# Sums of x2 with the rows of a1 and a3 for the last four token tiles: made in the second FFN group, one per item, in place of four at a time in the third

## The chip, the cores and the metric

The kernel runs on one core of one Trainium2 chip. The metric is the device time of one execution in microseconds (us). Its engines work side by side, each through its own queue in order: PE (TensorE, matrix products; PEld is its loading of weights), DVE (VectorE), ACT (ScalarE), POOL (GpSimd) and SP, which here starts nearly all DMAs.

## The reference, cut to what matters

The input is x of shape 2 x 1024 x 1024, that is 2048 tokens of width 1024. Two blocks follow each other; the first (gate, up, top-k, down) ends in x1 below, and only the second is touched.

```python
x1 = layernorm(x + attn_block(x, w_gate, w_up, w_down))
def qlora(x, wq, A, B):               # rank 2
    return x @ tile(wq, (1, 4)).T + (x @ A.T @ B.T) * 0.5
gate = silu(qlora(x1, w1q, a1, b1)); up = qlora(x1, w3q, a3, b3)
out  = layernorm(x1 + qlora(gate * up, w2q, a2, b2))
```

The rank-2 term of gate and up needs x1 @ a1.T and x1 @ a3.T: for each token four sums of 1024 products, one for each row of a1 and a3. These "sums", 0.5 times the product included, are what the change moves, for the tokens of the last four tiles. The width-1024 input is also folded four times to width 256, since wq is tiled four times.

## The kernel before, in words

**Tiles and groups.** The 2048 tokens are 16 tiles (0 to 15) of 128 tokens, in four groups of four (0 to 3). x1, called x2 in the code, is kept in DRAM as x_d[t]. The FFN runs group by group (`ffn(g)`, L854 on; group 1 is the second FFN group, group 2 the third). The inner width 2752 is cut into eight blocks b of 344. In the second half of the kernel the trace has for each group an f1 stage (32 items, one for each block and tile) and an f2 stage (the second product and layernorm, four items).

**One f1 item** (`f1_mm`, L958 on) is: PE makes 14 matmuls (L981 to L984) into one of three pairs of PSUM banks; ACT makes the silu of the gate half (L987); DVE multiplies it with the up half (L988), which frees the PSUM pair, and multiplies the product with two rows of a2 into a buffer pa (L990); ACT sums both halves of pa (L992, with its short reads of the accumulator); from block 2 on POOL adds the product to hf (L994).

**Preparing a tile for the next group** (`f1_tile`, L915 on) comes at the start of the even blocks, a tile each: SP loads x2 (L920); for tiles 12 to 15 alone, four times, DVE multiplies x2 with a row of a1 or a3 into a buffer pr (L925) and ACT sums it into `dall` (L926); POOL folds x2 (L927 to L929); DVE makes small copies of the four sums (L931 to L940). `f1_tile2` later transposes the result on PE (L949, L951). For the other tiles the sums come from the stages before the FFN (`dots_down`, `f1_first`).

**Buffers.** pr and pa share one tag with two buffers (`tag="pr", bufs=2`), given out in the order of the source. x2a has two buffers, gt three, PSUM pairs three.

**Order of the work.** `item` (L150 on) keeps a short line of pending items, so that the code of an item's matmuls follows four steps behind the step that calls it in the f1 stage. A planner of the framework (`schedule_with_timeline_sim=True`) then places the instructions on the queues from a timeline of its own, with the order of the source as preference. What an engine finds in its queue is then run strictly in that order.

Of the kernel before, what the change touches and what calls it, by code (L numbers as in the profile page):

```python
# [7 lines left out]
F = mybir.dt.float32  # L8
# [5 lines left out]
ALU = mybir.AluOpType  # L14
AF = mybir.ActivationFunctionType
# [3 lines left out]
P = 128  # L19
H = 1024  # L20
# [12 lines left out]
GT = 4  # L33
# [32 lines left out]
class Kern:  # L66
# [748 lines left out]
    def dots_down(self):  # L815
# [6 lines left out]
                self.nc.sync.dma_start(ab[i], self.A[("a1", "a3")[i // 2]][i % 2 : i % 2 + 1, :].partition_broadcast(P))  # L822
        yield from self.dots(range(2 * GT), [xt[:, 0:H], xt[:, H : 2 * H]], ab, jk[:, :H])

    def dots(self, tiles, xs, ab, jk):
        def load(t):
            with self.load_behind():
                self.nc.sync.dma_start(xs[t % 2], self.x_d[t])

        load(tiles[0])  # L830
        for t in tiles:
            for i in range(4):
                yield
                if i == 0 and t + 1 in tiles:
                    load(t + 1)
                with self.behind():
                    self.nc.vector.scalar_tensor_tensor(
                        jk, xs[t % 2], 0.5, ab[i], ALU.mult, ALU.mult, accum_out=self.dall[:, t, i : i + 1]
                    )
# [14 lines left out]
    def ffn(self, g):  # L854
        tiles = [t for t in range(g * GT, (g + 1) * GT) if t < self.nt]
        for b in range(NB):
            ws = []
            if tiles[-1] + 1 < self.nt:
                if b % 2 == 0:
                    if b:  # L860
                        self.f1_tile2(tiles[-1] + b // 2)
                    self.f1_tile(tiles[-1] + 1 + b // 2)
            for t in tiles:
                self.item(
                    lambda: self.f1_prep(b, ws),
                    lambda: None,
                    lambda st=self.fst[t], b=b, ws=ws: self.f1_mm(st, b, ws),
                    2, 2,
                )
        if tiles[-1] + 1 < self.nt:  # L870
            self.f1_tile2(tiles[-1] + GT)
        ws = []
        for t in tiles:
            self.item(
                lambda: self.f2_w(ws),
                lambda t=t: self.f2_prep(self.fst[t], t),
                lambda st=self.fst[t], t=t, ws=ws: self.f2_mm(st, t, ws),
                2, 1,
            )
# [35 lines left out]
    def f1_tile(self, t, f=None):  # L915
        nc, fp, sm = self.nc, self.fp, self.sm
        V, G = nc.vector, nc.gpsimd
        st = self.fst[t] = {}
        x2 = fp.tile([P, H], F, tag="x2a", bufs=2, name="x2a")
        nc.sync.dma_start(x2, self.x_d[t])  # L920
        d = self.dall[:, t]
        f = f or fp.tile([P, 2 * P], F, tag="fold", bufs=1, name="fold")
        for i in range(4 if t >= 3 * GT else 0):
            pr = self.fp2.tile([P, H], F, tag="pr", bufs=2, name="pr")
            V.tensor_tensor(pr, x2, self.abc[:, i, :], ALU.mult)  # L925
            nc.scalar.activation(pr, pr, AF.Copy, scale=0.5, accum_out=d[:, i : i + 1])  # L926
        G.tensor_tensor(f, x2[:, 0:256], x2[:, 256:512], ALU.add)  # L927
        G.tensor_tensor(f, f, x2[:, 512:768], ALU.add)
        G.tensor_tensor(f, f, x2[:, 768:1024], ALU.add)  # L929
        dr = sm.tile([P, 4], R, tag="dr", name="dr")  # L930
        V.tensor_copy(dr, d)  # L931
        tl = fp.tile([P, P + 6], F, tag="tl", bufs=1, name="tl")
        G.memset(tl, 0.0)
        d2 = d.rearrange("p (w r) -> p w r", w=2)
        dr2 = dr.bitcast(F).rearrange("p (w r) -> p w r", w=2)
        for w in range(2):
            q = 38 * w
            V.tensor_copy(tl[:, q : q + 2], dr2[:, w])
            V.tensor_copy(tl[:, q + 2 : q + 4], dr2[:, w])
            V.tensor_tensor(tl[:, q + 4 : q + 6], d2[:, w], dr2[:, w], ALU.subtract)  # L940
        st["f"] = f, tl
# [150 lines left out]
```

## Time and profile before

| what | us |
|---|---|
| median of 3 runs (lowest to highest) | 1923.47 (1922.35 to 1924.25) |
| the profiled execution: its own time | 1926.91 |
| the profiled execution: span from the first instruction to the last | 1925.1 |
| f1 stage of group 1, first matmul to last (1589.2 to 1662.7) | 73.5 |
| f1 stage of group 2 (1696.9 to 1775.4) | 78.5 |
| f1 stage of group 3 (1810.6 to 1882.7) | 72.1 |
| L925, the sums on DVE (128 x 1024), 16 of them: lowest / median / highest | 1.209 / 1.219 / 1.953 |
| L926, the sums on ACT, 16 of them: median, and 0.186 for the read of the accumulator | 1.060 |
| L994, POOL's add to hf, 96 of them: lowest / median / highest | 0.904 / 1.612 / 1.913 |

A page of the profile gives busy time by engine, and groups of instructions by source line. A timeline lists single instructions: start, duration, engine, line, operation, tiles, and in brackets how long the engine had been idle and what it waited for. "Waits" add such idle time up by pairs. "Windows" give busy time of each engine in a stretch. Durations of neighbours on one engine can overlap by some hundredths of a us, so the step from start to start is the better measure of what an instruction costs its queue.

### The profile page before, as it was taken

Reading aid. Unit: us, or ns where it says so; the run is one execution under the profiler, and the core shown is the slowest. Engines: PE = TensorE matmul, PEld = TensorE weight load, DVE = VectorE, ACT = ScalarE, POOL = GpSimd, SP = SyncE. Lnnn points to the kernel's source line nnn. Section 1 sums busy time; section 2 is a strip of 40 time slices with the busy share of each in tenths; the row PEclk is TensorE's granted clock in tenths of the full one; section 3 lists DMA queues with packets and bytes.
Section 4 is the critical chain, followed back from the end, with each engine's and each line's share of the span. In section 5 each row is a group of like instructions: output and inputs, shape, how many; then the busy total and the mean of one; then the engine's idle time right before and its main releaser. Section 6 shows DMA issues by size and latency. Waiting matters only on the chain. (4 is left out here: it accounts for less than half of the span.)

```text
span 1925.1 us, 29381 instructions
## 1 busy us (share of the span) xinstructions
PE 1885.3 (98%) x10825; PEld 1754.4 (91%) x10825; DVE 1229.6 (64%) x1831; ACT 904.0 (47%) x1448; POOL 973.0 (51%) x606
## 2 busy tenths in 40 slices
PE   9999999999999999999999999999998999998998
PEld 9999999999999999999888787888787979898896
DVE  4633556767358574691238998688467857779565
ACT  4333477414883258622246533323333746557362
POOL 5655664445445354355565443554565746436062
PEclk9999999999999999999999999999999999999999
DMA  7677687676977868667798756977776878485651
GB/s 266 237 250 260 236 325 261 210 272 253 330 231 241 314 235 303 236 228 256 282 328 285 270 188 227 337 245 261 268 250 244 279 284 321 155 318 177 229 196 66
DMA packets 166205, 488.66 MB, mean 254 GB/s; under 512 B 24772, under 2 KB 45380, under 8 KB 166056
## 3 DMA queue, kind: packets, MB, share of 16 engines
q1 hardware_dynamic: 165848, 486.43, 71.9%
q8 instruction: 85, 1.39, 0.3%
q14 instruction: 64, 0.52, 0.1%
q10 hardware_dynamic: 208, 0.31, 0.0%
HBM read 370.30 MB, written 116.33 MB: 253 GB/s over the span
## 5 line engine op out<-in xcount | busy, mean ns | idle before, releaser
L174 POOL TENSOR_TENSOR wl<-wr,wh 128x1376 fp32r<-128x1376 f32 (+2 forms) x187 | 566.4, 3035 | 466.1 <-ACT wh L173 436.8
L353 PE MATMUL mm<-wh,xh 128*128 128x344 f32 x1928 | 610.4, 322 | 2.8 <-DMA wh<-tw3T1h 2.8
L353 PE MATMUL mm<-wh,xl 128*128 128x344 f32 x1928 | 609.8, 320 | 0.0
L173 ACT CAST wh<-wr 128x1376 fp32r<-128x1376 f32 (+2 forms) x192 | 232.4, 1215 | 340.9 <-PE mm L353 199.6
L353 PEld LDWEIGHTS mm<-wh,xh 128*128 128x128 f32 x1928 | 364.7, 189 | 3.0 <-issue 3.0
L353 PEld LDWEIGHTS mm<-wh,xl 128*128 128x128 f32 x1928 | 364.6, 189 | 0.0
L353 PE MATMUL mm<-wl,xh 128*128 128x344 f32 x1928 | 342.1, 319 | 0.0
L353 PEld LDWEIGHTS mm<-wl,xh 128*128 128x128 f32 x1928 | 310.1, 188 | 0.0
L765 PE MATMUL mm<-wh,mh 128*128 128x512 f32 x680 | 217.8, 400 | 0.1
L765 PE MATMUL mm<-wl,mh 128*128 128x512 f32 x680 | 215.1, 395 | 1.1 <-POOL wl L174 1.1
L765 PE MATMUL mm<-wh,ml 128*128 128x512 f32 x648 | 205.5, 396 | 0.8 <-DVE ml L750 0.8
L460 ACT ACTIVATE jk<-a,cur 128x2752 int8<-128x2752 f32 x66 | 170.8, 2588 | 31.2 <-DVE cur L482 15.8
L994 POOL TENSOR_TENSOR hf<-hf,gt 128x344 f32<-128x344 f32 x96 | 142.2, 1491 | 75.6 <-DVE gt L988 68.7
L725 POOL TENSOR_TENSOR m<-m,ub 128x512 f32<-128x512 f32 (+2 forms) x93 | 111.0, 1194 | 128.0 <-ACT ub L724 65.8
L981 PE MATMUL mm<-wh,fh 128*128 128x344 f32 x512 | 166.2, 325 | 5.8 <-DVE gt L988 5.2
L983 PE MATMUL mm<-wh,fl 128*128 128x344 f32 x512 | 164.0, 320 | 0.0
L982 PE MATMUL mm<-wl,fh 128*128 128x344 f32 x512 | 163.9, 320 | 0.0
L765 PEld LDWEIGHTS mm<-wl,mh 128*128 128x128 f32 x680 | 127.4, 188 | 30.1 <-POOL wl L174 2.2
L768 DVE TENSOR_TENSOR acc<-acc,mm 128x1024 f32<-128x1024 f32 x96 | 116.4, 1214 | 57.9 <-PE mm L765 27.8
L765 PEld LDWEIGHTS mm<-wh,mh 128*128 128x128 f32 x680 | 124.7, 189 | 24.8 <-ACT mh L749 0.5
L765 PEld LDWEIGHTS mm<-wh,ml 128*128 128x128 f32 x648 | 121.2, 189 | 26.9 <-DVE ml L750 1.0
L992 ACT ACTIVATE pa<-pa 128x344 f32<-128x344 f32 x256 | 123.0, 483 | 38.6 <-DVE pa L990 34.0
(191 smaller groups left out, 2742.5 us busy)
## 6 DMA issues: line engine op xcount, KB each, us to landing
wr<-wu SPq DMA_DIRECT2D x64, 688.0 KB
wr<-wg SPq DMA_DIRECT2D x52, 688.0 KB
wr<-wd SPq DMA_DIRECT2D x48, 512.0 KB
s_d<-cc SPq DMA_DIRECT2D x64, 344.0 KB
m_d<-mt SPq DMA_DIRECT2D x64, 344.0 KB
a<-s_d SPq DMA_DIRECT2D x64, 344.0 KB
wl<-wc_w SPq DMA_DIRECT2D x48, 344.0 KB
wh<-wc_w SPq DMA_DIRECT2D x48, 344.0 KB
```

Of the source, the lines that this page charges most:

```text
L173: self.lasta = self.nc.scalar.copy(hi, raw)
L174: (eng or self.nc.gpsimd).tensor_tensor(lo, raw, hi.bitcast(F), ALU.subtract)
L353: self.nc.tensor.matmul(o, l, r, start=start and n < m and n % (2 * KH) == 0, stop=stop and n >= m and (n - m) % KH == KH - 1)
L460: nc.scalar.activation(jk.bitcast(I8), av[j], AF.Sign, bias=t, scale=-1.0, accum_out=s)
L725: nc.gpsimd.tensor_tensor(m[:, :w], m[:, :w], ub[:, :w], ALU.mult)
L765: nc.tensor.matmul(ps[:, h], a, b[:, h * 512 : (h + 1) * 512], start=i == 0, stop=i == len(ops) - 1)
L768: nc.vector.tensor_tensor(out, out, ps.rearrange("p a b -> p (a b)"), ALU.add)
L981: nc.tensor.matmul(o, fh[:, c, :], wh[:, c, :], start=c == 0, stop=False)
L982: nc.tensor.matmul(o, fh[:, c, :], wl[:, c, :], start=False, stop=False)
L983: nc.tensor.matmul(o, fl[:, c, :], wh[:, c, :], start=False, stop=False)
L992: nc.scalar.activation(pa[:, r], pa[:, r], AF.Copy, scale=0.5, accum_out=part[:, r, b : b + 1])
L994: G.tensor_tensor(hf[:, hs], hf[:, hs], gt, ALU.add)
```

## The change

The four sums leave `f1_tile`. A generator `dots3` makes them: for each tile from 12 on it loads x2 into an x2a buffer, and with each call makes one sum, a product on DVE and a sum on ACT as before. It is created at the start of block 0 of group 1, and called once before each item of the odd blocks; four odd blocks with four items each make the 16 sums. `f1_tile` for tiles 12 to 15, in group 2, still loads x2 for the folds.

```diff
+    def dots3(self):
+        for t in range(3 * GT, self.nt):
+            x2 = self.fp.tile([P, H], F, tag="x2a", bufs=2, name="dx")
+            self.nc.sync.dma_start(x2, self.x_d[t])
+            for i in range(4):
+                d, pr = self.dall[:, t, i : i + 1], self.fp2.tile([P, H], F, tag="pr", bufs=2, name="pr")
+                self.nc.vector.tensor_tensor(pr, x2, self.abc[:, i, :], ALU.mult)
+                self.nc.scalar.activation(pr, pr, AF.Copy, scale=0.5, accum_out=d)
+                yield
...
+            if (g, b) == (1, 0):
+                self.dg = self.dots3()
             for t in tiles:
+                if b % 2:
+                    next(self.dg, None)
                 self.item(
...
         f = f or fp.tile([P, 2 * P], F, tag="fold", bufs=1, name="fold")
-        for i in range(4 if t >= 3 * GT else 0):
-            pr = self.fp2.tile([P, H], F, tag="pr", bufs=2, name="pr")
-            V.tensor_tensor(pr, x2, self.abc[:, i, :], ALU.mult)
-            nc.scalar.activation(pr, pr, AF.Copy, scale=0.5, accum_out=d[:, i : i + 1])
```

## The prediction, made before the changed kernel was built

> **What bounds the kernel.** I read the page first, then the windows of the f1 stages of groups 1, 2 and 3, then PE's waits and the timelines of DVE, POOL and ACT in them. The page:
>
> ```profile
> span 1925.1 us, 29381 instructions
> PE 1885.3 (98%) x10825; PEld 1754.4 (91%) x10825; DVE 1229.6 (64%) x1831; ACT 904.0 (47%) x1448; POOL 973.0 (51%) x606
> ```
>
> PE bounds the kernel; only idle time of PE can be won or lost. The three f1 stages, in order (stretch, its length, busy time of PE, PEld, DVE, ACT, POOL, granted clock, DMA share, GB/s):
>
> ```profile
> 1589.20:1662.70 73.50, 73.50 (x473) 73.20 (x472) 53.93 (x104) 47.44 (x157) 47.94 (x43) 1.00 0.77 276
> 1696.90:1775.40 78.50, 74.87 (x473) 73.23 (x472) 72.31 (x110) 59.38 (x180) 43.03 (x37) 1.00 0.73 245
> 1810.60:1882.70 72.10, 72.10 (x459) 71.89 (x458) 47.17 (x76) 45.55 (x155) 37.81 (x26) 1.00 0.65 228
> ```
>
> Groups 1 and 2 make the same matmuls (x473). Group 1 does it in 73.5 us with PE never idle; group 2 takes 78.5, and its DVE is busy for 72.3 of them. In group 2 PE waits (total, times, longest):
>
> ```profile
> PE mm L981 <- DVE gt L988: 3.6, 5, 1.7
> ```
>
> The rest of the 5.0 us is the pipeline running dry and refilling at five stalls. The sums stand right there. DVE at the last of the four bursts:
>
> ```profile
> 1749.56 1.95 DVE L925 TENSOR_TENSOR pr<-x2a,abc 128x1024 f32<-128x1024 f32 x1
> 1751.43 0.50 DVE L988 TENSOR_TENSOR gt<-gt,mm 128x344 f32<-128x344 f32 x1
> 1751.85 3.09 DVE L925 TENSOR_TENSOR pr<-x2a,abc 128x1024 f32<-128x1024 f32 x2
> 1754.86 0.50 DVE L988 TENSOR_TENSOR gt<-gt,mm 128x344 f32<-128x344 f32 x1
> 1755.28 1.21 DVE L925 TENSOR_TENSOR pr<-x2a,abc 128x1024 f32<-128x1024 f32 x1
> 1756.42 1.60 DVE L990 TENSOR_TENSOR pa<-gt,ab 128x688 f32<-128x688 f32 x1
> 1757.94 0.50 DVE L988 TENSOR_TENSOR gt<-gt,mm 128x344 f32<-128x344 f32 x1
> ```
>
> and POOL beside it:
>
> ```profile
> 1752.00 1.85 POOL L994 TENSOR_TENSOR hf<-hf,gt 128x344 f32<-128x344 f32 x1 [1.58 <-DVE gt L988]
> 1755.44 1.85 POOL L994 TENSOR_TENSOR hf<-hf,gt 128x344 f32<-128x344 f32 x1 [1.59 <-DVE gt L988]
> ```
>
> POOL's add takes 0.904 alone but 1.85 here, and L990 1.60 in place of its usual 0.87: one waits while the other runs. With DVE's queue full, each add of POOL costs DVE about 0.75 (1.60 less 0.87). Now DVE and POOL in group 1, undisturbed:
>
> ```profile
> 1643.27 0.51 DVE L988 TENSOR_TENSOR gt<-gt,mm 128x344 f32<-128x344 f32 x1 [0.78 <-ACT gt L987]
> 1643.81 0.87 DVE L990 TENSOR_TENSOR pa<-gt,ab 128x688 f32<-128x688 f32 x1
> 1645.47 0.52 DVE L988 TENSOR_TENSOR gt<-gt,mm 128x344 f32<-128x344 f32 x1 [0.78 <-ACT gt L987]
> ```
>
> ```profile
> 1643.86 1.61 POOL L994 TENSOR_TENSOR hf<-hf,gt 128x344 f32<-128x344 f32 x1 [0.59 <-DVE gt L988]
> ```
>
> An item takes PE 2.20 us (1643.27 to 1645.47). DVE needs 1.42 and idles 0.78, but POOL's add runs in that very gap: it ends at 1645.47.
>
> **What is removed.** Twelve of the 16 sums lie inside group 2's f1 stage, four (1666 to 1671) in the f2 stage of group 1. Without them group 2's f1 stage should run as group 1's does now: 78.5 - 73.5 = **5.0 us won**. The four in f2 hide nothing: PE has no idle time after 1663.8 there, so they give back 0. PE also waits 0.8 for DVE (L1029) as group 2's f2 begins; I count it as 0 and keep 0.8 for the range. ACT's 12 x (1.06 + 0.19) go too; no wait of PE names them.
>
> **What is added.** Sixteen products on DVE and sixteen sums on ACT, all in group 1's f1 stage. With the line of pending items, the sums of block 1's calls stand before items of block 0, and so on: tile 12 in block 0, 13 in block 2, 14 in block 4, 15 in block 6. The order of pr and pa pins them: in group 2 the pa of item 4 (L990) came only after the burst, though its L988 had run.
>
> One product steps DVE's queue by 1.14 (1755.28 to 1756.42): 16 x 1.14 = 18.2. In blocks 2, 4 and 6, 12 products stand beside a POOL add, 12 x 0.75 = 9.0. Together 27.2 against DVE's idle time in that stage, 73.5 - 53.9 = 19.6. So 7.6 are lacking. Some of this is queue: how late may L988 be before PE stops? At 1734.10 PE had waited 1.75, for an L988 that I put 5.05 late (started 1733.55, its item's matmuls done at 1727.9, usual delay 0.6): PE tolerates **3.3**. 7.6 - 3.3 = 4.3.
>
> The same walked item by item: L988, product and L990 with POOL's add take 3.08 (1754.86 to 1757.94), so each item of a called block falls 0.88 behind; the first falls 0.75 + 1.14 - 0.78 = 1.1, as the gap is POOL's. Four: 3.7, which is 0.4 over; in the next block DVE regains 2.20 - 1.33 = 0.87 per item and is level. So 0.4 for each of blocks 4 and 6, 1.4 for block 2 (L988 begins there at 1614.1 after a gap of 1.9 and three more follow closely; the fourth would stand 3 x 3.22 later, 3.22 being L988's step 0.54, L990's 0.79, POOL's 0.75 and the product's 1.14, and end at 1624.3, where PE needs its pair at 1636.1 - 6 x 2.20 = 1622.9, counted back from the steady items), and an estimate of 0.9 for block 0, where DVE is already busy with the last layernorm of group 0 (9.0 of 10 us from 1590). Sum 3.1; folds of POOL that come later, as tiles 9 to 11 now have one x2a buffer in turn with `dots3`, add about 0.8 (one more wait of 0.75). I take **4.2 lost**, near both 4.3 and 3.9; the ends are 0 (all fits the gaps) and 7.6 (no queue to draw on).
>
> ACT: 1.30 an item in steady state, 2.4 with a sum, against 2.20; 0.8 over four items, below DVE's lag. The new loads: four of 0.5 MB. SP's queue now waits at them for a free x2a buffer, with the weights of the next block behind; those have a block of 8.8 us in hand, so 0; without that cover, the price of rival three. Tile 13's load waits for tile 12's products (about 1603) and its first product stands at about 1609; in group 1 an x load issued at 1582.8 let DVE go on at 1588.5, 5.7 later. It just fits.
>
> A rule of the Trainium skill bears on POOL's waits. "SBUF — State Buffer", section "Who interferes with whom", says that a DVE instruction with two SBUF inputs and a GpSimd instruction that reads SBUF exclude each other for the whole instruction, whoever begins first. The rows agree with exclusion (L990 0.87 or 1.60), but by the rule the price would be a whole add, 0.90 for 0.75: 12 x 0.15 = 1.8 more lost, an estimate from that page. "Perfetto Trace Analysis", section "Optimizing Scalar/DVE Operations", says that where DVE causes bubbles though it is not saturated, smaller pieces help; by that the loss would be near 0, but no run here shows it, and group 1's DVE would be close to saturated.
>
> **Sum.** -5.0 + 4.2 = -0.8 on the profiled execution, 1926.91 to 1926.1 (its span and the 1.8 around it). It stands 3.4 above the median of the runs; the same difference on 1923.47 gives **1922.7**.
>
> **Rivals.**
>
> 1. *Fits the gaps, faster.* If products fall where POOL is not waiting, an item takes 1.33 + 1.14 = 2.47 and falls 0.27 behind; four make 1.1, far below 3.3, and PE never stops. For it: DVE has 19.6 idle. Against: POOL's add fills that gap in every steady item. Loss 0 to 1: net -4 to -5, and -5.8 with f2's 0.8. About 1919.0.
>
> 2. *ACT in the wrong order, slower.* If the planner puts the sum of an item (L926) ahead of the silu (L987) of the item whose PSUM pair PE needs, each late product holds the silu: 1.14 + 1.15 (ACT) + 0.46 (L987) + 0.51 (L988) + 0.79 (L990) + 0.75 (POOL) = 4.8 an item. The lag is 2.8, then 2.6 each, 10.6 less 3.3 = 7.3 in each of three blocks and about 4 in block 0: 26 lost, net +21; if half the items stand so, +8. It decides where the product ends after its item's matmuls. For it: the order at 1751.5 is L926 before L987, twice. Against: in steady items ACT idles 0.80 until the matmuls of an item end, so that its silu is ready before a late product is. 1931 to 1944.
>
> 3. *Late load, slower.* Tile 13's or 14's x2 lands after DVE has reached its product; L988 stands behind. 5.7 less the lag PE bears, twice: +5, about 1928.5.
>
> 4. *Nothing moves.* Pinned by the pr order, the sums could run later than meant; the bursts then stay bursts, and the time stays within 1 us of before.
>
> **Chances.** My case 0.42; rival one 0.27; rival two 0.24; rival three 0.05; rival four 0.02. A measurement of this kernel can tell about 0.2%, 3.8 us, from no change. My case and rival four are within it (0.44), rival one faster (0.27), two and three slower (0.29). The range goes from 5.8 won, 1917.7, to 1938, which leaves out the worse half of rival two (0.12) and little below. The likeliest case's own range, from its ends (0 to 7.6 lost), is 1918.5 to 1926.1.
>
> **What would show it.** L925 at 16 places in 1590 to 1660 and none after 1665; group 2's f1 stage at 73.5; DVE in group 1's f1 stage near 72 busy; L990 and L925 there near 1.6 and 1.9 beside L994; PE waiting for L988 in blocks 0, 2, 4 and 6. I am wrong if PE has no idle time in group 1 (rival one), if ACT waits for L925 with a silu behind (two), or if L925 waits for a DMA (three).

## Result, and the profile after

The changed kernel takes 1929.64 us (median of 6 runs, 1924.01 to 1932.12) against 1922.91 for the kernel before (6 runs, 1919.90 to 1924.25). The ratio is 1.0034, with a 95% interval of 1.0019 to 1.0049: the change costs 6.7 us. 1922.7 was predicted, with a gain of 0.8.

The page of the profile after:

```profile
span 1922.2 us, 29388 instructions
PE 1883.6 (98%) x10825; PEld 1754.0 (91%) x10825; DVE 1227.5 (64%) x1831; ACT 903.8 (47%) x1448; POOL 975.6 (51%) x606
```

**A trap comes first.** This profiled execution took 1924.01, which is 2.9 *less* than the profiled execution of before, though the medians say 6.7 more. The part ahead of the FFN differs: the first L994 matmul of group 0 (L984 before) starts at 1462.82, against 1471.57, with the same instructions in the same order on every engine, the semaphore records apart. In the 14 profiled executions of this study that part takes between 1462.8 and 1471.6. So two whole spans can't be compared here, but two FFNs can. From that matmul to the end it is 453.53 before and 459.38 after, 5.85 more, close to the 6.7 of the medians. All stage lengths below run from the first to the last L994 of the stage (f1) and from there to the first one of the next (f2).

| kernel | f1.0 | f2.0 | f1.1 | f2.1 | f1.2 | f2.2 | f1.3 | f2.3 | FFN |
|---|---|---|---|---|---|---|---|---|---|
| before | 79.80 | 38.79 | 72.24 | 35.47 | 77.23 | 36.41 | 70.84 | 42.75 | 453.53 |
| after | 80.02 | 38.45 | 80.78 | 38.60 | 72.28 | 35.50 | 70.84 | 42.91 | 459.38 |
| difference | +0.2 | -0.3 | **+8.5** | **+3.1** | **-4.95** | **-0.9** | 0 | +0.2 | +5.85 |

"f1.1" is the f1 stage of group 1. The gain in group 2 is there, 5.9 with f2; the loss in group 1 is 11.7, where 4.2 was forecast. Here are the windows of the f1 stages of groups 1, 2 and 3, as in the prediction, with group 1's f2 stage as the second line (stretch, length, busy time of PE, PEld, DVE, ACT, POOL, granted clock, DMA share, GB/s):

```profile
1580.30:1662.70 82.40, 76.11 (x474) 73.16 (x473) 78.38 (x125) 61.13 (x183) 45.16 (x42) 1.00 0.80 278
1662.70:1699.70 37.00, 34.32 (x152) 27.60 (x152) 20.03 (x52) 10.45 (x30) 7.44 (x16) 0.95 0.41 145
1699.70:1773.30 73.60, 73.60 (x473) 73.21 (x472) 50.36 (x95) 47.00 (x157) 44.39 (x38) 1.00 0.74 256
1807.50:1879.70 72.20, 72.20 (x460) 71.94 (x459) 47.21 (x76) 45.57 (x155) 37.88 (x26) 1.00 0.66 227
```

Group 2 now runs as group 1 did before (73.6, PE never idle). Group 1 is worse than group 2 ever was: 82.4, with DVE busy for 78.4 of it. PE's waits in that f1 stage:

```profile
PE mm L991 <- DVE gt L998: 4.9, 6, 1.6
PE tp L959 <- POOL fold L939: 1.2, 1, 1.2
```

and in the f2 stage behind it:

```profile
PE mm L765 <- ACT hh L1038: 2.7, 1, 2.7
```

The same wait for hh was 0.76 before. It is the last items of f1, late, that f2 needs. The wait of 1.2 ended by a fold is POOL's lateness in its own right: the last fold of tile 9 began only at 1609.8, among adds, as its x2 had come late (POOL waited 9.0 for it).

Now DVE in block 6 of group 1, where one product goes with each item (start, duration, engine, line, operation):

```profile
1645.86 1.75 DVE L831 TENSOR_TENSOR pr<-dx,abc 128x1024 f32<-128x1024 f32 x1
1647.54 0.50 DVE L998 TENSOR_TENSOR gt<-gt,mm 128x344 f32<-128x344 f32 x1
1648.13 0.99 DVE L1000 TENSOR_TENSOR pa<-gt,ab 128x688 f32<-128x688 f32 x1
1649.04 1.95 DVE L831 TENSOR_TENSOR pr<-dx,abc 128x1024 f32<-128x1024 f32 x1
1650.91 0.50 DVE L998 TENSOR_TENSOR gt<-gt,mm 128x344 f32<-128x344 f32 x1
1651.52 1.63 DVE L1000 TENSOR_TENSOR pa<-gt,ab 128x688 f32<-128x688 f32 x1
1653.08 1.21 DVE L831 TENSOR_TENSOR pr<-dx,abc 128x1024 f32<-128x1024 f32 x1
```

and POOL in the same stretch ("x2" puts two adds together):

```profile
1646.49 3.42 POOL L1004 TENSOR_TENSOR hf<-hf,gt 128x344 f32<-128x344 f32 x2
1651.49 0.93 POOL L1004 TENSOR_TENSOR hf<-hf,gt 128x344 f32<-128x344 f32 x1 [1.58 <-DVE gt L998]
```

No line of DVE has a bracket: it waits for no other engine's result, one instruction follows the other. Yet L831 takes 1.75 and 1.95 in place of 1.21, and L1000 1.63 in place of 0.87. The second of POOL's two adds ends at 1649.91, inside the product that starts at 1649.04 and takes 0.74 too long; the add of 1651.49 runs undisturbed in 0.93, and the L1000 that starts with it, at 1651.52, takes 0.76 too long. The product of 1653.08 meets no add and takes 1.21. From one L998 to the next it is 3.37 and 3.3, where PE's item takes 2.20. ACT beside it:

```profile
1647.65 1.06 ACT L832 ACTIVATE pr<-pr 128x1024 f32<-128x1024 f32 x1 [0.56 <-DVE pr L831]
1648.61 0.19 ACT L832 ACTIVATION_READ_ACCUMULATOR pr<-pr 128x1 f32 x1
1648.70 0.44 ACT L997 ACTIVATE gt<-mm 128x344 f32<-128x344 f32 x1
```

The sum (L832) does stand before a silu (L997), as rival two feared. But that silu ends at 1649.14, and DVE comes to its next L998 only at 1650.91: DVE is later still.

### The profile page after: what moved, and what is told of

Its sections match the earlier page's. It is cut to its first block, busy times and chain, and to the rows that moved or that the text cites. A ratio compares the mean times of both kernels' runs of the same rounds, so it can differ in the third digit from the quotient of the medians.

```text
span 1922.2 us, 29388 instructions
## 1 busy us (share of the span) xinstructions
PE 1883.6 (98%) x10825; PEld 1754.0 (91%) x10825; DVE 1227.5 (64%) x1831; ACT 903.8 (47%) x1448; POOL 975.6 (51%) x606
## 5 line engine op out<-in xcount | busy, mean ns | idle before, releaser
L174 POOL TENSOR_TENSOR wl<-wr,wh 128x1376 fp32r<-128x1376 f32 (+2 forms) x187 | 568.6, 3047 | 471.8 <-ACT wh L173 459.9
L1004 POOL TENSOR_TENSOR hf<-hf,gt 128x344 f32<-128x344 f32 x96 | 141.8, 1487 | 73.5 <-DVE gt L998 71.8
L765 PEld LDWEIGHTS mm<-wh,mh 128*128 128x128 f32 x680 | 124.3, 188 | 24.5 <-ACT mh L749 0.4
```

Source lines behind the costliest of these rows:

```text
L174: (eng or self.nc.gpsimd).tensor_tensor(lo, raw, hi.bitcast(F), ALU.subtract)
L765: nc.tensor.matmul(ps[:, h], a, b[:, h * 512 : (h + 1) * 512], start=i == 0, stop=i == len(ops) - 1)
L1004: G.tensor_tensor(hf[:, hs], hf[:, hs], gt, ALU.add)
```

## Experiments

Theories at the start. **B**: products of DVE and adds of POOL keep each other out, so that the 12 sums beside adds (blocks 2 to 7) each cost about 1 us. **A**: the x2a buffers, now shared with `dots3`, push the folds of tiles 9 to 11 late (they run at 1602 to 1611, 1625 to 1630 and 1642 to 1647), and late folds put POOL, and then DVE, behind. **C**: ACT, as in rival two. Diffs are against the changed kernel, but for the eleventh. Each stage length is from one profiled execution. The changed kernel has two (after and e12): f1.1 differs by 1.1 between them and f2.1 by 0.95, so single differences of about 1 us say nothing. The ratio is to the kernel before, with its 95% interval.

| run | ratio | f2.0 | f1.1 | f2.1 | f1.2 | f2.2 | FFN |
|---|---|---|---|---|---|---|---|
| before | 1 | 38.79 | 72.24 | 35.47 | 77.23 | 36.41 | 453.53 |
| after | 1.0034 [1.0019, 1.0049] | 38.45 | 80.78 | 38.60 | 72.28 | 35.50 | 459.38 |
| e1 no sums | 0.9990 [0.9977, 1.0002] | 39.88 | 74.07 | 35.48 | 72.27 | 35.52 | 451.75 |
| e2 own x2 buffer | 1.0094 [1.0071, 1.0116] | 38.95 | 94.4 | 37.24 | 72.28 | 35.53 | 471.56 |
| e3 one SBUF input | 1.0018 [1.0005, 1.0031] | 38.97 | 76.57 | 39.04 | 72.27 | 35.50 | 456.16 |
| e4 sum on DVE | 1.0022 [1.0012, 1.0032] | 40.89 | 80.50 | 40.13 | 72.29 | 35.47 | 462.12 |
| e5 x2 in the weight ring | 1.0053 [1.0034, 1.0073] | 40.92 | 83.80 | 40.42 | 72.27 | 35.53 | 465.58 |
| e6 no POOL add | 0.9962 [0.9948, 0.9976] | 38.86 | 72.64 | 33.95 | 72.29 | 35.50 | 446.75 |
| e7 bursts of four | 1.0016 [1.0006, 1.0026] | 39.09 | 78.44 | 38.02 | 72.85 | 35.51 | 456.65 |
| e8 sums in f2 | 1.0066 [1.0051, 1.0081] | 39.49 | 82.96 | 40.39 | 72.30 | 35.53 | 465.4 |
| e9 split | 0.9976 [0.9965, 0.9986] | 38.76 | 73.87 | 35.47 | 72.44 | 35.52 | 449.32 |
| e10 split, weight ring | 0.9984 [0.9975, 0.9994] | 39.72 | 75.08 | 35.49 | 72.27 | 35.53 | 450.9 |
| e11 no POOL add, before | 0.9987 [0.9976, 0.9999] | 38.74 | 72.48 | 33.93 | 74.61 | 37.07 | 450.37 |
| e12 after, again | 1.0032 [1.0018, 1.0047] | 38.91 | 81.87 | 37.65 | 72.28 | 35.51 | 459.9 |

### 1. The gain alone: no sums at all

```diff
-                self.dg = self.dots3()
+                self.nc.gpsimd.memset(self.dall[:, 3 * GT :, :], 0.0)
...
-                if b % 2:
-                    next(self.dg, None)
```

> Leaves out the 16 sums of the last four tiles altogether (they are set to 0), in both places. Measures what taking them out of group 2 brings by itself. Both theories: group 2's f1 stage at 72.2 to 72.4 us from the first L994 to the last (77.2 before the change, 72.3 after it) and group 1's at 72.2 as before the change; time 5 to 6 us under the kernel before (ratio 0.997). If the ratio stays at 1.000, the stages of the profile do not add up to the time.

Measured: 0.9990. f1.2 and f2.2 gain just what they gain in the changed kernel (-4.96 and -0.9), and group 1 is near its old time. So nearly all of the loss in group 1 is the sums' own. The whole, -1.8 in the profile, misses the 5 to 6 expected, as f1.0, f2.0 and f1.1 are each 1.1 to 1.8 longer here. In f1.1 it is one stall of 1.58 at 1623.5, where DVE had stood behind POOL's memset of tl. In f2.0 the granted clock is 0.50 for 6.8 us (from 1554.1), where it is so for 3.4 us in the kernel before. In f1.0 PE waits 6.8 in place of 4.4; why, isn't known.

### 2. Theory A: another buffer for the new loads

```diff
-            x2 = self.fp.tile([P, H], F, tag="x2a", bufs=2, name="dx")
+            x2 = self.fp2.tile([P, H], F, tag="x2", bufs=2, name="dx")
```

> The changed kernel with the x2 of the sums loaded into the two buffers of f2's x2, so that the folds keep both x2a buffers. Theory A (the folds of POOL came late through the shared x2a buffers, into the blocks where POOL also adds, and each costs DVE a wait of about 0.75): six to nine folds go back ahead of block 2, group 1's f1 stage falls from 80.8 to 75 to 77 and the time by 4 to 6 us against the changed kernel. Theory B (the products and POOL's adds alone fill DVE): f1 stage still 79 to 81. Theory C (ACT's sums hold the silu): as B.

Measured: 1.0094, worse, and by a new mechanism. The buffer x2 is also that of the f2 stage, here group 0's; the first product runs only at 1607.4, and the pa of the first items stand behind it on DVE, so that PE stood for 13.5 us at one place. This run says nothing on A, as f1.1 is another stage altogether; experiment 5 tries another buffer.

### 3. Theory B: a product with a single SBUF input

DVE halves x2 and sums it in one instruction, without the rows of a1 and a3.

```diff
-                self.nc.vector.tensor_tensor(pr, x2, self.abc[:, i, :], ALU.mult)
+                self.nc.vector.tensor_scalar(pr, x2, 0.5, None, ALU.mult, ALU.add, accum_out=d)
```

> The changed kernel with each product made as x2 times 0.5, an operation with one input from SBUF (the row of a1 or a3 is left out, so the sums are others). Same number of instructions on DVE, ACT, POOL. Theories A and B (DVE and POOL exclude each other when DVE reads two inputs from SBUF): no product is stretched beyond 1.3 us by POOL, the adds of POOL beside them go from 1.85 to about 0.95, group 1's f1 stage falls to 75 to 77. Theory C (ACT) or plain length of DVE's work: 80 to 81 as in the changed kernel.

Measured: f1.1 is 4.2 shorter than after (76.57), f2.1 is 39.04, as late as after; 1.0018. DVE's groups in the f1 stage of group 1 (busy us, mean ns | idle before), in the profile after:

```profile
L1000 DVE TENSOR_TENSOR pa<-gt,ab 128x688 f32<-128x688 f32 x22 | 25.8, 1174 | 0.8
L831 DVE TENSOR_TENSOR pr<-dx,abc 128x1024 f32<-128x1024 f32 x15 | 23.9, 1592 | 0.0
```

The same two groups in this run:

```profile
L1000 DVE TENSOR_TENSOR pa<-gt,ab 128x688 f32<-128x688 f32 x22 | 27.6, 1258 | 0.9 <-ACT pr L832 0.2
L831 DVE TENSOR_SCALAR_CACHE_REDUCE pr<-dx 128x1024 f32<-128x1024 f32 x15 | 18.1, 1207 | 0.0
```

and pa alone in the changed kernel's second profile (experiment 12):

```profile
L1000 DVE TENSOR_TENSOR pa<-gt,ab 128x688 f32<-128x688 f32 x21 | 26.3, 1258 | 0.7
```

From the changed kernel to this one the products lose their stretch altogether (1592 to 1207 ns). So half of B holds: a product with two SBUF inputs waits for POOL, one with a single input doesn't. The multiplication into pa, untouched by the edit, keeps its stretch. Its mean is higher than in the profile after (1258 against 1174), but the unaltered kernel's second profile has 1258 too; that waiting passes from the products on to pa isn't shown. The Trainium skill, "SBUF — State Buffer", section "Who interferes with whom", has this very distinction: a DVE instruction with two SBUF inputs contends with a GpSimd instruction that reads SBUF, one with a single input, outside the two-port modes, doesn't. The means here agree with it (1592 against 1207).

### 4. Theory C: the sum without ACT

```diff
-                self.nc.vector.tensor_tensor(pr, x2, self.abc[:, i, :], ALU.mult)
-                self.nc.scalar.activation(pr, pr, AF.Copy, scale=0.5, accum_out=d)
+                self.nc.vector.scalar_tensor_tensor(pr, x2, 0.5, self.abc[:, i, :], ALU.mult, ALU.mult, accum_out=d)
```

> The changed kernel with each sum made on DVE alone (product and sum in one instruction, about 1.22 plus 0.08 by L837), nothing on ACT. Theory C (ACT's 1.15 per sum holds the silu or the buffers of pr): group 1's f1 stage falls from 80.8 to 76 or less. Theories A and B: 80 to 82, since DVE has 16 times 0.08 more and waits for POOL as before.

Measured: f1.1 80.50 against 80.78, and the whole 1.0022, with an interval that overlaps that of after. ACT without a single sum leaves f1.1 where it was, so C falls, and rival two with it.

### 5. Theory A again: x2 in the ring of weight buffers

```diff
-            x2 = self.fp.tile([P, H], F, tag="x2a", bufs=2, name="dx")
+            x2 = self.wr.get()[:, :H]
```

> The changed kernel with the x2 of the sums loaded into the ring wr, which is idle after group 0, so that the folds keep both x2a buffers and no load of the sums waits for f2. Theory A (folds of POOL that came late cost DVE waits): POOL makes the folds of tiles 9 to 12 ahead of block 3 again, group 1's f1 stage falls from 80.8 to 76 to 78, time 3 to 5 us under the changed kernel. Theory B (products against POOL's adds alone): 79.5 to 81.

Measured: 1.0053; f1.1 is 83.80, longer than after by 3.0, though the folds, which no longer wait for a buffer that `dots3` holds, all lie between 1592.9 and 1614.4. So early folds don't bring the time back. The run doesn't say more than that: the first products now stand beside folds and are stretched as well (1.70 to 1.76 at 1595.1 and 1601.9), and 1.1 of the 3.0 is no more than lies between the changed kernel's two profiles. What settles A is experiment 6.

### 6. Theory B: no adds of POOL in group 1

Items of group 1 leave out POOL's add to hf.

```diff
-        st = self.fst[t] = {}
+        st = self.fst[t] = {"add": t // GT != 1}
...
-        if b >= 2:
+        if b >= 2 and st.get("add", True):
```

> The changed kernel without POOL's add to hf in group 1 (the output of group 1's tokens lacks six of eight blocks). Theory B (each add costs DVE about 0.75 beside a product; 12 of them 9.0): group 1's f1 stage falls from 80.8 to 73 to 75 and the wait at the start of its f2 (2.7) to about 0.8. Theory A (folds alone): 77 to 79. If neither, and DVE is short of time by itself: 79 or more.

Measured: 0.9962. f1.1 is 72.64, as short as before, with all its products in it. DVE's groups in that stage:

```profile
L1000 DVE TENSOR_TENSOR pa<-gt,ab 128x688 f32<-128x688 f32 x22 | 20.2, 921 | 1.0 <-ACT pr L832 0.2
L831 DVE TENSOR_TENSOR pr<-dx,abc 128x1024 f32<-128x1024 f32 x15 | 19.4, 1291 | 0.0
```

The window of the whole stage (columns as above):

```profile
1585.00:1658.00 73.00, 73.00 (x469) 72.59 (x468) 68.38 (x129) 61.17 (x187) 14.95 (x20) 1.00 0.91 312
```

PE is never idle while DVE is busy for 68.4 of 73.0: the products do fit, as long as POOL doesn't take its turns (it is busy 15 instead of 45). The folds are as late here as in the profile after (those of tiles 9 to 11 begin at 1606.5, 1622.0 and 1638.9), and no matmul waits for them: late folds alone cost nothing, so A falls as the main cause. Only together with the adds do they show, in one wait of PE of 1.24 for a fold (after and e12). Leaving the adds out might shorten the stage without any sums too; experiment 11 asks that.

### 7. Four sums at a time

```diff
-                if b % 2:
+                for _ in range(4 if b % 2 and t == tiles[0] else 0):
                     next(self.dg, None)
```

> The changed kernel with the four sums of a tile made before the first item of the odd block, not one before each item. Tells whether spreading them helps. If a burst costs 2.5 per tile beside POOL's adds, as in group 2 before the change, and nothing in the first two blocks: group 1's f1 stage at 78 to 80, that is no worse than spread (80.8). If spreading is what keeps PE going: 83 or more.

Measured: f1.1 and f2.1 together 116.5, against 119.4 (after) and 119.5 (again after, experiment 12); 1.0016. One sum per item was no better than four at a time, by these profiles worse by 2.9 (the ratios can't tell, their intervals overlap). The median product takes 1231 ns here and 1748 ns after. The place of the products has its part in that: the burst of tile 12 runs at 1553.6 to 1561 in group 0's f2, that of tile 13 at 1605.2 to 1610.8, as POOL's adds begin (1609.7). Eight products stand among the adds, where after has eleven. So this run doesn't separate bursts from places.

### 8. The sums in the f2 stages of groups 0 and 1

```diff
-            if (g, b) == (1, 0):
+            if (g, b) == (0, 7):
                 self.dg = self.dots3()
...
+            for _ in range(2 if g < 2 else 0):
+                next(self.dg, None)
```

(x2 lies in the weight ring here, and the calls in the f1 items are gone.)

> The sums made in the f2 stages of groups 0 and 1, two before each of the eight f2 items, with x2 in the ring wr. DVE is busy for about half of f2 and POOL makes no adds there. Theories A and B: f1 stages of groups 1 and 2 both at 72.3 to 74, f2 stages up by 0 to 1.5 each; time 2 to 5 us under the kernel before the change. If f2 has no room either (its layernorm and transposes wait for DVE): f2 of group 0 and 1 up by 3 or more each, and no gain.

Measured: 1.0066. f2.0, f1.1 and f2.1 take 162.8, against 146.5 before. In f2 PE now waits 3.6 for hl (L1039, two waits, the longest 2.7), which it does not before; its waits for hh (3.4 in all) are as before (3.6). I take from it that f2 has no free place for them. That f1.1 grew as well, to 82.96, is mostly a matter of the border: 30 matmuls of group 0's second product that lie in f2.0 in the kernel before run behind the first L994 of group 1 here. f2.0 and f1.1 together are 122.5, against 111.0 before.

### 9. Half of them, where no add runs

POOL's adds begin with block 2. Eight sums (tiles 14 and 15) go to the items of group 1 that run ahead of that; those of tiles 12 and 13 stay in group 2's `f1_tile`.

```diff
-        for t in range(3 * GT, self.nt):
+        for t in range(3 * GT + 2, self.nt):
...
-                if b % 2:
+                if g == 1 and 0 < b < 3:
                     next(self.dg, None)
...
+        for i in range(4 if 3 * GT <= t < 3 * GT + 2 else 0):
+            pr = self.fp2.tile([P, H], F, tag="pr", bufs=2, name="pr")
+            V.tensor_tensor(pr, x2, self.abc[:, i, :], ALU.mult)
+            nc.scalar.activation(pr, pr, AF.Copy, scale=0.5, accum_out=d[:, i : i + 1])
```

> Half of the change: the sums of tiles 14 and 15 in group 1, one before each item of blocks 0 and 1, where POOL makes no adds (calls in blocks 1 and 2); those of tiles 12 and 13 left in group 2's f1_tile, where the bursts cost nothing before the change. Theory B (products cost time only beside POOL's adds): f1 stage of group 1 at 72.3 to 74, of group 2 at 72.3 to 73; time 3 to 5 us under the kernel before the change, ratio 0.998. If DVE in blocks 0 and 1 of group 1 is full with group 0's last layernorm: f1 of group 1 at 75 or more and no gain.

Measured: 0.9976 (0.9965 to 0.9986), 1917.45 us: faster than both kernels. The products of group 1 run from 1556.1 to 1612.6, POOL's first add at 1611.6; those of group 2 from 1664.3 to 1712.3, its first add at 1719.9. f1.1 is 73.87 (+1.6 to before) and f1.2 72.44 (-4.8). DVE's groups in group 1's f1 stage:

```profile
L1004 DVE TENSOR_TENSOR pa<-gt,ab 128x688 f32<-128x688 f32 x23 | 23.7, 1041 | 0.7
...
L831 DVE TENSOR_TENSOR pr<-dx,abc 128x1024 f32<-128x1024 f32 x7 | 9.3, 1335 | 0.2 <-ACT pr L832 0.2
```

(L1004 is the pa of this kernel.) Both are below after's 1174 and 1592. The run halves the number of sums in group 1 and changes their place at once; that it is the adds that matter rests on experiments 6 and 11.

### 10. The split, with x2 in the weight ring

Experiment 9 with `x2 = self.wr.get()[:, :H]` in `dots3`.

> As e9_split, with the x2 of the sums in the ring wr. The folds then come as early as before the change, into blocks 0 and 1 beside the products. Theory B with folds counted as POOL's work like the adds: f1 stage of group 1 one to three us longer than in e9_split. If folds do not matter: the same.

Measured: 0.9984, f1.1 75.08. f1.1 is 1.2 longer than in experiment 9, at the low end of what was expected if folds count like adds, but so much lies between two profiles of one kernel, and the intervals overlap: these runs can't tell the two buffers apart.

### 11. The control for experiment 6

The edit of experiment 6, on the kernel before.

> The kernel before the change without POOL's add in group 1 (the output of group 1's tokens lacks six of eight blocks). A control for e6_no_add: with no sums in group 1 the adds cost PE nothing, so its f1 stage stays at 72.2 and its f2 at 34 to 35.5; group 2 as before the change at 77.2. If the f1 stage here falls below 72, the adds cost time without the sums too, and e6 shows less than it seems.

Measured: f1.1 72.48 and f2.1 33.93, against 72.64 and 33.95 in experiment 6. So without adds the 16 products cost 0.16 in f1 and 0.02 in f2; with adds they cost 8.5 and 3.1. The whole loss of 11.7 needs both sides. (Group 2's f1 was expected at 77.2 and came out at 74.61, though its adds are all there; why, wasn't followed.)

### 12. The changed kernel again

Unaltered, on the chip of experiments 9 to 11.

> The changed kernel once more, on the chip of these runs, with a second profile: f1 and f2 of group 1 at 80 to 82 and 38 to 39.5, group 2's at 72.3 and 35.5, ratio 1.003 to 1.004. It tells how far stages differ from run to run; more than 2 us would make the other comparisons loose.

Measured: 1.0032. f1.1 and f2.1 make 119.52, after had 119.38. One by one they are 81.87 and 37.65, against 80.78 and 38.60, f2.1 a little below the range expected. Each execution has one stretch of 3.4 us in which the granted clock is 0.50, in f2.1 after and in f1.1 here (from 1616.4); the last section comes back to it.

## Why the prediction was wrong, step by step

**What bounds the kernel: right.** PE's idle time decides, and all of the difference lies in the two groups named.

**The gain: right.** 5.0 forecast, 4.95 measured; the 0.8 at group 2's f2, which I kept for the range alone, came too (0.9).

**Where the sums run: right.** The first product of tile 12 at 1551.1, still beside group 0's f2, the others of tile 12 at 1588.6, 1592.5 and 1595.3 in block 0; tile 13 at 1604 to 1615, tile 14 at 1624 to 1636, tile 15 at 1646 to 1656. Twelve in the blocks of POOL's adds, as I had put it; the first of them, at 1604.0, was ahead of the first add (1605.7).

**The loss: 4.2 forecast, 11.7 measured.** This is the failing step, and in it two terms: the 3.3 taken off for the queue, and DVE's idle time, taken as wholly free. The terms of its sum, beside what the profile after has (DVE, f1 stage of group 1; waiting is counted by the mean step, up to the next instruction's start with idle time left out, as durations of neighbours overlap):

| term | forecast | measured | from |
|---|---|---|---|
| products | 18.2 | 17.1 | 15 x 1.14; one ran before the stage |
| more waiting for POOL | 9.8 | 9.9 | L831: 15 x (1.523 - 1.14) = 5.7; pa: 22 x (1.076 - 0.883) = 4.2 (L1000 after, L990 before) |
| DVE idle time that they fill | 19.6 | 15.6 | 82.40 - 78.38 = 4.0 is left idle |
| lacking | 8.4 | 11.4 | |
| queue that PE draws on | -3.3 | 0 | f2 is 3.1 longer |
| loss | 5.1 | 11.7 (f1 8.5, f2 3.1) | |

(Of the forecast's 9.8, 9.0 was for the adds and 0.8 for the folds; the 4.2 that was taken lies between the results of its two ways, 3.9 and 4.3. The 11.4 and the 11.7 need not agree to a tenth. DVE's busy time in the stage grew by 24.5, 78.38 less 53.93, not by the 27.0 of products and waiting, mostly because one item less of DVE's work lies in the stage, 22 of L1000 for 23 of L990; and part of f2's 3.1 is the clock, see 1.)

1. *The queue, 3.3.* I took off what PE tolerates as if it were a gift. It is a loan: a lag that is there at the end of f1 is asked for at the start of f2, where PE waits 2.7 for hh instead of 0.76. That f2.1 is 3.1 longer, nearly the 3.3, is partly luck: 1.9 is the longer wait, and the other 1.2 goes with a granted clock of 0.50 behind it. In experiment 12, where the clock stayed at 1.00 in f2.1, it is 2.2 longer than before. The walk item by item made the same mistake: it took only what went over 3.3 in a block as lost, and let the next block work off the rest.
2. *Idle time, 4.0.* Not all of DVE's 19.6 can be had. In the stage after, DVE still waits 2.8 for others: 1.1 for POOL's memset of tl, 0.7 for a short step of the layernorm on POOL, 1.0 for ACT. The other 1.2 is the short gaps between instructions (1.4 before: 19.6 less waits of 18.2).

*The waits* were right in size. The price of one is 0.74 to 0.76 (1.95 against 1.21, 1.63 against 0.87), where 0.75 was forecast, and the sum is 9.9 for 9.8. Their place was not: I had put them to the products and the folds, and 4.2 of the 9.9 stands at pa. One term stood for something else: the 0.8 for late folds was to be one more wait of DVE; what shows is PE's own wait of 1.24 for a fold.

That the products and POOL's adds cost this only together is shown by experiments 6 and 11: with the same products and no adds the loss is 0.2. DVE had just about the room for the work; it had none for the waits.

**ACT at nothing: right.** Its lag stays below DVE's, as the prediction had it, even where a sum stands ahead of a silu; experiment 4 takes all sums from it and leaves f1.1 at 80.50.

**The loads at nothing: right for DVE.** In that stage DVE waits for no DMA. The one that it waits for just ahead of it, group 0's last x, is the same as before (6.4, before 6.1). POOL does wait: 9.0 for the x2 of tile 9, and that is how its folds came late.

**The rivals.** One, "fits the gaps", fell by what spoke against it; its condition, products that meet no add, is just what experiments 6 and 9 made. With the split, which moves half of the sums, the FFN is 4.2 shorter and the time 1917.45; rival one's 1919.0 was for moving all of them. Two fell with experiment 4. Three wasn't seen in the changed kernel; the stall in experiment 2 is of its kind, an instruction waiting for its data with pa queued behind. Four fell: f1.2 lost its bursts.

The two rules of the Trainium skill that the prediction weighed: by "SBUF — State Buffer", section "Who interferes with whom", a wait would be a whole add, 0.90, an estimate; the rows give 0.74 to 0.76. By "Perfetto Trace Analysis", section "Optimizing Scalar/DVE Operations", breaking up instructions may help where DVE causes bubbles without being saturated; no run here breaks a product up.

**What stays open**: why f1.0 grew in experiment 1, why f1.1 is 83.80 in experiment 5, and what makes the part ahead of the FFN vary by 8.8 from one profiled execution to another.

## What to carry to other kernels

Before work is moved into an engine's idle time, ask what else runs in that gap: here DVE's gap was POOL's turn, and the moved work cost 0.2 without POOL's adds and 11.7 with them. A tolerance (a queue, spare buffers) shifted the lag to the next stage here; take it off a loss only where that stage can absorb it. And look for a place of the same stage where the rival isn't at work: half of the sums in blocks 0 and 1, ahead of the adds, brought 0.24%, where all of them, one per item, lost 0.34%.

## What the runs showed of the hardware

**The granted clock fell after waits of PE of 2 to 3.4 us, nearly each time, and after a few shorter ones.** After PE's 2.7 in f2 of the profile after (stretch, length, busy times, then the clock, DMA share, GB/s):

```profile
1665.40:1667.00 1.60, 1.60 (x4) 1.26 (x5) 1.60 (x5) 1.05 (x5) 1.00 (x2) 0.50 0.80 318
1667.00:1669.00 2.00, 2.00 (x9) 1.63 (x8) 1.25 (x3) 0.94 (x4) 0.23 (x1) 0.62 0.11 36
1669.00:1671.00 2.00, 2.00 (x10) 1.63 (x9) 0.86 (x2) 0.59 (x3) 0.00 (x0) 1.00 0.54 157
```

From 1665.1 to 1668.5 PE has a clock of 0.50, then 1.00 again (the second line holds both). From group 0's f2 to group 3's f1 the 14 profiled executions have 22 waits of PE between 2.1 and 3.4 us, and such a stretch goes with 21 of them; the one without is the 2.67 at the start of f2.1 in experiment 12. Of twelve waits between 1.2 and 1.8 it goes with two (1.24 in experiment 12, 1.71 in experiment 5). The stretches there last 3.41 us or a multiple of it, and from start to start they are whole numbers of 3.41 us apart (1545.6 and 1665.1 after: 35). So where a wait falls on that grid may decide; that isn't shown. The price can be read off the changed kernel's two profiles: in f2.1 PE is busy for 35.9 with the stretch and 34.7 without, in f1.1 for 75.9 with it and 74.5 without, 1.2 to 1.4 us a time. The Trainium skill, "TensorE: Matmul & The Clock Gate", section "What's actually happening", puts the threshold at an idle window of about 3.4 us, and says that the window runs free. The lengths and starts of the stretches agree with a free-running window of 3.4 us; but waits shorter than that brought the clock down here.

In the stall of 13.5 us of experiment 2 the mean clock of ten of its us was 0.64:

```profile
1620.00:1630.00 10.00, 0.00 (x0) 0.00 (x0) 9.43 (x15) 7.95 (x28) 5.40 (x5) 0.64 0.55 169
```

**DVE's instructions that read two tiles from SBUF waited for POOL, and those that read one didn't.** In one f1 stage the 128 x 1024 product took 1592 ns on average with two inputs and 1207 with one (experiment 3). One wait was 0.74 to 0.76 us beside an add of 0.93 us. pa, which kept its two inputs, kept its stretch: 1258 ns in experiment 3, 1174 and 1258 in the two profiles of the changed kernel.
